# Attention's value products on four 32-column tiles of TensorE in place of two 64-column tiles

## The chip, the cores and the metric

The kernel runs on one core of a Trainium2 chip. The metric is the device time of one execution, in microseconds (us). A core has five engines that run side by side and wait for one another by semaphores: PE (TensorE, the matrix engine; its weight loads have a row of their own, PEld), DVE (VectorE), ACT (ScalarE), POOL (GpSimd) and SP (SyncE, which here issues the DMAs).

## The reference

The input `x` has 64 batches of 256 nodes with 512 features; `adj` is a graph on the 256 nodes. Two layers follow each other, and each adds its result to its input and normalises over the features.

```
# layer 0: one step on the graph
out = deg * (x @ Wi.T + b) + adj @ (x @ Wj.T)
h   = layernorm(x + out)
# layer 1: attention with 8 heads of 64 features, masked by the graph
q, k, v = split_heads(h @ Wq.T + bq), ..., ...
attn = softmax(where(adj == 0, -inf, q @ k.T / 8))
out  = layernorm(h + (attn @ v) @ Wo.T + bo)
```

The change touches the product `attn @ v` alone. It is computed here as exponentials times `v`, and divided by the sums of the exponentials afterwards.

## The kernel before

**Groups and slots.** Batches are worked on in pairs; 32 pairs make 32 groups `g`. Within a group the attention runs over 8 units `w`: `i, pr = divmod(w, 4)` gives the batch of the pair and a pair of heads. The loop takes two units at a time, which I call a slot, so a group has four slots. In all groups but the last, a slot runs on PE in this order, written out by hand and kept as written (`in_order`, `keep_in_program_order`):

1. `values(g, w)` and `values(g, w + 1)`: the products into the tile `pav`. This is what the change edits.
2. `divide`: four products of `ones` with `pk` into `den`, which sum the exponentials of each head over the keys.
3. `scores`: the products of `qT` and `kT` into `ps` for the next units, in the first three slots. In the fourth, the projections of the group's end (`st`) follow.
4. Pieces of the next group's layer 0 (`po`, `pa`), which fill PE while the other engines make the exponentials.

All matrix products go through one helper, so the profile gives them line L290, and they are told apart by the tile that they write. A product of 32-bit floats stands in the trace as two `MATMUL` and two `LDWEIGHTS` records.

**The tile shapes.** PE's array of 128 by 128 can be used as several smaller arrays. The profile writes the shape in use as rows*columns:

- `po`, `st` and `pa` use the whole array, `128*128`.
- `pav` uses `128*64`: head `j` of the pair writes partitions `64j` to `64j + 63`, so the heads `j = 0` and `j = 1` stand on two tiles of the array. One unit is 2 chunks of keys (`kc`) times 2 heads: 4 products, each with 128 keys as rows, 64 features as columns, and 256 queries that stream.
- `den` uses `128*32`: its four products of 32 columns stand on four tiles, placed by `tile_position=(0, q * R)` with `R = 32`.
- `ps` uses `64*128`: two tiles one above the other, since a head has 64 features.

**What hangs on these products.** ACT makes the exponentials `pe` (L813) after DVE has added the mask (L809), and POOL adds the two halves of `pe` to `pk` (L816), which `den` reads. When `pav` of a slot is complete, ACT copies it to `aoT` (L853). When `den` is complete, DVE takes its reciprocal `rden` (L886). SP then issues 8 DMAs that spread `rden` over the partitions, and POOL multiplies `aoT` by it one slot later (L848). `pav` has one PSUM bank (`ps_v`, 1 buffer). `den` shares three banks with `po` and `st` (`ps_m`).

**The group's end.** After the fourth slot's `den` come the output projection (`st<-factor,aoT` and `st<-factor,oS`), and then the query, key and value projections of the next group (`st<-hT`, `st<-hS`). DVE turns `h` there (`hT<-hB`, a transpose of data that came back by DMA), and sums blocks of it.

**The last group** has no next layer 0 to mix in. It takes single units, with `scores` between them, and for its last two units `divide_at_once` computes `den` on `128*64` tiles.

Of the kernel before, what the change touches and what calls it, by code (L numbers as in the profile page):

```python
# [16 lines left out]
P = 128  # L17
# [207 lines left out]
def unshifted_path(ctx, tc, flag, x, adj, wiT, wjT, b0, wqT, bq, wkT, bk, wvT, bv, woT, bo, out):  # L225
# [18 lines left out]
    NT = N // P  # L244
    NC = D // P
    DH = 64
    R = 32
# [30 lines left out]
    def value_bank(name):  # L278
        return ps_v.tile([P, 512], F32, tag="av", name=name)


    def in_order(ins):

        tc.keep_in_program_order(ins)
# [4 lines left out]
    def matmul(*args, **kw):  # L289
        in_order(nc.tensor.matmul(*args, **kw))  # L290
# [33 lines left out]
    xT, xS, hT, hS, qT, kT, vv, aoT, oS = ({} for _ in range(9))  # L324
# [310 lines left out]
    def pair_blocks(m, tag):  # L635

        s = p1.tile([P, 4, 2, N], F32, tag=tag, name=tag)
        return left_blocks(m[:, 0:2, 0:N], m[:, 2:4, 0:N], m[:, 0:2, N:2 * N], m[:, 2:4, N:2 * N], s)
# [33 lines left out]
    def second_late(steps):  # L672
        return [steps[0], steps[2], steps[1], *steps[3:]]
# [30 lines left out]
    def qk_steps(g, store, tag, bias, diff, early=False):  # L704

        def new_store():
            store[g] = p1.tile([P, NC, NB * N], F32, tag=tag, name=tag)

        def place(i, j):
            return store[g][:, 2 * j:2 * j + 2, i * N:(i + 1) * N]  # L710

        def biased(b):
            def evict(dst, ps):
                for m in range(2):
                    nc.scalar.activation(dst[:, m, :], ps[:, m, :], AF.Identity, bias=b[:, m:m + 1], scale=1.0)
            return evict

        def last(dst, ps, addend):
            for m in range(2):
                nc.vector.scalar_tensor_tensor(dst[:, m, :], ps[:, m, :], diff[:, m:m + 1],  # L720
                                               addend[:, m, :], ALU.add, ALU.add)

        return qkv_steps(g, True, new_store, place, biased(bias), biased(diff), last, early)
# [98 lines left out]
    pavs = {}  # L822
# [7 lines left out]
    def values(g, w):  # L830
        i, pr = divmod(w, NC)
        if w == 0:
            aoT[g] = p1.tile([P, NC, NB * N], F32, tag="aoT", name="aoT")
            oS[g] = pair_blocks(aoT[g], "oS")
        pp = w % 2
        if pp == 0:
            pavs[g] = value_bank("pav").rearrange("p (r q) -> p r q", r=2)
        pe, _ = made[g, w]
        for kc in range(NT):
            for j in range(2):  # L840
                h0 = (2 * pr + j) * DH
                matmul(pavs[g][j * DH:(j + 1) * DH, pp, :], vv[g][:, i, kc, h0:h0 + DH], pe[:, j, kc, :],
                       start=(kc == 0), stop=(kc == NT - 1))

    def multiply():
        while products:
# [73 lines left out]
    def order_of(name):  # L920
        return [(name, n) for n in RIGHT]

    for g in range(-1, NG - 1):
        o, q, k, v = (order_of(name) for name in ("wo", "wq", "wk", "wv"))
# [18 lines left out]
    p, q = l0_steps(0), l0_steps(1)  # L943
# [42 lines left out]
    for g in range(NG - 1):  # L986
# [4 lines left out]
        for w in range(2, NB * NC, 2):  # L991
            values(g, w - 2)
            values(g, w - 1)
            multiply()
            divide_two(g, w - 1)
            scores(g, w)()
            if w == 4:
                run(work[2])
            later = scores(g, w + 1)
            later()  # L1000
            run(work[w // 2 if w < 4 else w // 2 + 1])
        w = NB * NC - 2
        values(g, w)
        values(g, w + 1)
        multiply()
        o = o_steps(g)
        q = second_late(qk_steps(g + 1, qT, "qT", bq_sb, bqd))
# [20 lines left out]
    g = NG - 1  # L1028
# [89 lines left out]
```

## Time and profile before

| | |
|---|---|
| median of 3 runs | 3089.34 us (3087.36 to 3089.66) |
| the profiled execution's own time | 3086.33 us |
| its span in the trace | 3084.3 us |
| PE busy | 3055.9 us, 99% of the span, 14598 `MATMUL` records |
| PEld busy | 2122.5 us, 69% |
| DVE, ACT, POOL busy | 71%, 32%, 49% |
| DMA engines busy | 48.9% |
| granted TensorE clock | 0.999 |

The profile comes from one execution, in which the time outside the span was 2.0 us. Its time is 3.0 us below the median of the three timed runs. Busy time of a group of instructions is the union of their durations: the records of `pav` last 386 ns each on average, but since they overlap, 2048 of them cover only 250.1 us. So the starts of records tell what a product costs on PE, and the mean duration of one does not.

### The profile page before, as it was taken

What the parts mean: (1) busy time and instruction counts of PE and PEld (TensorE: products, weight loads), DVE (VectorE), ACT (ScalarE), POOL (GpSimd) and SP (SyncE); (2) the same over time, 40 slices, a digit from 0 to 9 for tenths busy, and PEclk for the clock granted to TensorE, in tenths of its full rate; (3) what the DMA queues carried; (4) which work ended last, traced back from release to release, by engine and by line L of the source; (5) the groups of instructions that cost most, each with busy time, mean ns of one, the idle gap of its engine ahead of it and who ended that gap; (6) DMA issues with size and microseconds to landing.
All of it is one profiled execution on the core that took longest, in us unless ns stands there. A gap on an engine that the chain in (4) does not pass through costs nothing. (4 is left out here: it accounts for less than half of the span.)

```text
span 3084.3 us, 42714 instructions
## 1 busy us (share of the span) xinstructions
PE 3055.9 (99%) x14598; PEld 2122.5 (69%) x14598; DVE 2176.4 (71%) x3298; ACT 974.7 (32%) x1861; POOL 1519.8 (49%) x1255
## 2 busy tenths in 40 slices
PE   7999999999999999999999999999999999999998
PEld 4667766677766777666776667776677766677665
DVE  6777677766777667777667676677766777767765
ACT  2323333323333333332233332333332333323332
POOL 2544445544546445464454554454544546445453
PEclk9999999999999999999999999999999999999999
DMA  7355544455444555445554445544455444555333
GB/s 258 121 147 157 168 124 129 135 158 166 143 127 124 159 169 152 119 131 151 159 167 120 126 141 159 166 140 126 126 157 170 148 121 128 156 161 164 118 110 99
DMA packets 410395, 447.28 MB, mean 145 GB/s; under 512 B 40896, under 2 KB 300224, under 8 KB 409792
## 3 DMA queue, kind: packets, MB, share of 16 engines
q1 hardware_dynamic: 410176, 444.50, 48.9%
q8 instruction: 120, 1.97, 0.3%
q14 instruction: 99, 0.81, 0.1%
HBM read 340.79 MB, written 70.25 MB: 133 GB/s over the span
## 5 line engine op out<-in xcount | busy, mean ns | idle before, releaser
L461 POOL TENSOR_TENSOR rstd<-ve,mhalf 128x1 f32<-128x1 f32 x256 | 140.6, 553 | 706.2 <-DVE below L459 706.2
L816 POOL TENSOR_TENSOR pk<-pe 128x512 f32<-128x512 f32 x256 | 322.6, 1276 | 327.4 <-ACT pe L813 327.3
L290 PE MATMUL po<-w,xS 128*128 128x512 f32 x1024 | 463.0, 599 | 0.4 <-DVE xS L478 0.4
L290 PE MATMUL st<-hS,factor 128*128 128x256 f32 x2048 | 453.1, 379 | 1.6 <-DVE u L689 1.2
L290 PEld LDWEIGHTS st<-hS,factor 128*128 128x128 f32 x2048 | 387.9, 190 | 56.6 <-DVE u L689 1.7
L813 ACT ACTIVATE pe<-pe 128x1024 f32<-128x1024 f32 x256 | 270.8, 1058 | 379.0 <-DVE pe L809 379.0
L290 PE MATMUL po<-w,xT 128*128 128x512 f32 x768 | 351.9, 601 | 13.4 <-DVE xT L485 10.9
L290 PE MATMUL st<-hT,factor 128*128 128x256 f32 x1536 | 352.4, 379 | 0.7 <-ACT hT L626 0.7
L290 PEld LDWEIGHTS po<-w,xS 128*128 128x128 f32 x1024 | 189.7, 190 | 236.3 <-issue 207.2
L809 DVE TENSOR_TENSOR pe<-ps,maskT 128x1024 f32<-128x1024 f32 x256 | 297.9, 1194 | 35.3 <-PE ps L290 35.3
L290 PEld LDWEIGHTS st<-hT,factor 128*128 128x128 f32 x1536 | 291.5, 190 | 42.3 <-ACT hT L626 0.9
L886 DVE RECIPROCAL rden<-den 128x256 f32<-128x256 f32 x127 | 222.6, 1753 | 92.1 <-PE den L290 89.0
L887 POOL TENSOR_TENSOR rtot<-rtot,rden 128x256 f32<-128x256 f32 x127 | 106.9, 841 | 329.4 <-DVE rden L886 329.4
L290 PEld LDWEIGHTS po<-w,xT 128*128 128x128 f32 x768 | 143.6, 191 | 180.7 <-issue 162.5
L290 PE MATMUL ps<-qT,kT 64*128 64x256 f32 x2048 | 264.9, 392 | 0.0
L290 PE MATMUL pav<-pe,v_sb 128*64 128x256 f32 x2048 | 250.1, 386 | 1.9 <-ACT pe L813 1.8
L290 PEld LDWEIGHTS pav<-pe,v_sb 128*64 128x64 f32 x2048 | 135.3, 136 | 154.1 <-issue 95.5
L290 PEld LDWEIGHTS ps<-qT,kT 64*128 64x128 f32 x2048 | 184.3, 186 | 78.2 <-issue 51.3
L744 DVE TENSOR_TENSOR xh<-st,xh 128x512 f32<-128x512 f32 x186 | 144.5, 777 | 131.7 <-PE st L290 131.7
L290 PE MATMUL st<-factor,hS 128*128 128x256 f32 x1024 | 234.8, 382 | 0.0
L290 PE MATMUL st<-factor,oS 128*128 128x256 f32 x992 | 224.2, 379 | 0.0
L290 PEld LDWEIGHTS st<-factor,hS 128*128 128x128 f32 x1024 | 191.9, 190 | 35.4 <-issue 10.6
(115 smaller groups left out, 4633.5 us busy)
## 6 DMA issues: line engine op xcount, KB each, us to landing
xB<-in_x_dram SPq DMA_DIRECT2D x256, 128.0 KB, 3.9
xh<-in_x_dram SPq DMA_DIRECT2D x64, 512.0 KB, 4.3
factor<-wq SPq DMA_DIRECT2D x128, 256.0 KB, 4.2
factor<-wk SPq DMA_DIRECT2D x128, 256.0 KB, 2.8
factor<-wv SPq DMA_DIRECT2D x128, 256.0 KB, 2.7
spread<-rden SPq DMA_DIRECT2D x1016, 32.0 KB, 1.9
factor<-wo SPq DMA_DIRECT2D x124, 256.0 KB, 3.2
h_cols<-xh SPq DMA_DIRECT2D x124, 256.0 KB, 2.8
```

Source lines behind the costliest of these rows:

```text
L290: in_order(nc.tensor.matmul(*args, **kw))
L461: nc.gpsimd.tensor_tensor(rstd, ve, mhalf, ALU.pow)
L744: nc.vector.tensor_add(dst, src, dst)
L809: nc.vector.tensor_add(pe.rearrange("p j t q -> p j (t q)"), ps.rearrange("p j t q -> p j (t q)"), maskT.rearrange("p t q -> p (t q)").uns ...
L813: in_order(nc.scalar.activation(flat, flat, AF.Exp, scale=QSCALE, accum_out=etot[:, NB * g + i, pr:pr + 1]))
L816: nc.gpsimd.tensor_tensor(pk, pe[:, :, 0, :], pe[:, :, 1, :], ALU.add)
L886: nc.vector.reciprocal(rden, den)
L887: nc.gpsimd.tensor_tensor(rtot, rtot, rden, ALU.add)
```

## The change

In `values`, the loop over the two heads becomes a loop over four blocks of 32 columns. Block `q` holds 32 of the 64 features of head `q // 2`, and writes partitions `32q` to `32q + 31` of `pav`.

```
         for kc in range(NT):
-            for j in range(2):
-                h0 = (2 * pr + j) * DH
-                matmul(pavs[g][j * DH:(j + 1) * DH, pp, :], vv[g][:, i, kc, h0:h0 + DH], pe[:, j, kc, :],
-                       start=(kc == 0), stop=(kc == NT - 1))
+            for q in range(P // R):
+                d0 = 2 * pr * DH + q * R
+                matmul(pavs[g][q * R:(q + 1) * R, pp, :], vv[g][:, i, kc, d0:d0 + R], pe[:, q // 2, kc, :],
+                       start=(kc == 0), stop=(kc == NT - 1), tile_position=(0, q * R))
```

A unit now has 8 products of 32 columns where it had 4 of 64, each with the same 256 queries streaming; the two blocks of a head stream the same exponentials. Over the kernel, 1024 products become 2048. In the built programs nothing else differs: PE has every other product at its place, and DVE, ACT, POOL and SP have the same instructions in the same order. The edit reaches the last group as well, where `divide_at_once` keeps its 64 columns.

## The prediction

> **What bounds the kernel now.** I read the page's first part, then who PE waits for, then the timeline of one slot.
>
> ```profile
> span 3084.3 us, 42714 instructions
> PE 3055.9 (99%) x14598; PEld 2122.5 (69%) x14598; DVE 2176.4 (71%) x3298; ACT 974.7 (32%) x1861; POOL 1519.8 (49%) x1255
> ...
> L290 PE MATMUL pav<-pe,v_sb 128*64 128x256 f32 x2048 | 250.1, 386 | 1.9 <-ACT pe L813 1.8
> ```
>
> PE is busy for 99% of the span. The row of `pav`, the edited products, shows 1.9 us of idle time before 2048 records. The list of PE's waits adds up to 20 us, and its largest line is the kernel's start:
>
> ```profile
> PE po L290 <- DVE xT L485: 10.9, 2, 8.1
> PE pt_h L293 <- ACT xh L467: 2.3, 2, 1.2
> PE pav L290 <- ACT pe L813: 1.8, 2, 1.0
> ```
>
> So PE sets the time, and what its stream sheds or gains, the kernel sheds or gains, until another engine comes late. But a busy PE need not be streaming. The timeline of one slot (columns: start, length, then the group; the number after x counts records) shows what lies between starts:
>
> ```profile
> 1052.71 0.59 PE L290 MATMUL po<-w,xS 128*128 128x512 f32 x1
> 1053.24 1.95 PE L290 MATMUL pav<-pe,v_sb 128*64 128x256 f32 x16
> 1055.11 0.64 PE L290 MATMUL den<-pk,ones 128*32 128x256 f32 x8
> 1055.68 2.00 PE L290 MATMUL ps<-qT,kT 64*128 64x256 f32 x16
> ...
> ```
>
> And a stretch of whole-array products, then the end of the last group:
>
> ```profile
> 1006.16 1.89 PE L290 MATMUL st<-factor,aoT 128*128 128x256 f32 x8
> 1007.89 5.34 PE L290 MATMUL st<-factor,oS 128*128 128x256 f32 x24
> ...
> ```
>
> ```profile
> 3063.74 1.08 PE L290 MATMUL pav<-pe,v_sb 128*64 128x256 f32 x8
> 3064.66 1.03 PE L290 MATMUL den<-pk,ones 128*64 128x256 f32 x8
> ```
>
> Take starts, not lengths. Eight `st` records take 1007.89 - 1006.16 = 1.73 us, 216 ns each: 256 columns streamed twice. The 16 records of `pav` take 1055.11 - 1053.24 = 1.87 us. They run in pairs, one for each half of the array, so they make 8 steps, and 8 x 0.216 = 1.73 us. The 8 records of `den` run four at once, make 2 steps (0.43 us), and take 0.57. So `pav` and `den` each carry 0.14 us that is no streaming. In the last group, `pav` and `den` both stand on 64 columns: 3064.66 - 3063.74 = 0.92 us for 4 steps (0.86), only 0.06 over, though output, weights and data all change there.
>
> The single records of the slot tell the extra time apart (ns, from start to start; outside the last group each repeats within 2 ns):
> - Within `pav`: 267 for the first step, then 216 for each. Products of one step start 7 apart.
> - From the last start of `pav` to the first of `den`: 309 in all 127 places, so 93 more than a step. The same 93 stands from `den` to `ps` and from `st` to `ps`, and 90 from `ps` to `po`: wherever the shape changes. From `pav` to the 64-column `den` it is 210.
> - Within `den`: 240 for its first step.
>
> **What the Trainium skill says.** "TensorEngine Tiling (Array Packing)", section Key Properties: "Changing tiling mode (not just tile) drains the TensorE". The trace agrees: 93 ns at each change of shape, nothing without one. "TensorE: Matmul & The Clock Gate", section LDWEIGHTS (loading the stationary operand): a load takes as long as its columns divided by 1.2 per ns, so 53 ns for 64 columns and 27 for 32 as estimates from that page. The trace's first steps are longer by 51 and 24 ns: after a change the second load finds no stream to hide behind. The same page, section The mechanism, has tiles of the array running at once, about 4 ns apart; here it is 7. Its section Measured speedup vs the span model reports 2.38 times for three tiles of 32 columns, one product each; no run here shows that, nor a long run of fours.
>
> **The change, part by part.**
>
> *Streaming.* Each product covers a quarter of the array's columns where it covered half, and there are twice as many: 8 products of two records per unit, 32 records per slot, in fours 8 steps as before. If four run at once, streaming costs the same 8 x 216 ns; nothing is gained there.
>
> *First step.* After the change of shape from `po`, the exposed load is of 32 columns: 240 instead of 267. That removes 27 ns.
>
> *From pav to den.* Both are now `128*32`: no drain. Step to step is 216 where last `pav` to first `den` was 309. As the last record of a four starts 20 ns after its first, and of a pair 7, count from first records: 316 before, 216 after. That removes 100 ns.
>
> *Den's first step* has its loads hidden behind the last `pav` step: 216 instead of 240. That removes 24 ns.
>
> *From den to ps* (or to `st` in the fourth slot): the change of shape stays, 309.
>
> The sum is 27 + 100 + 24 = 151; by whole slots, from `pav`'s first start to `ps`'s: 2446 before; after, 240 + 8 x 216 + 20 + 309 = 2297, so 149 ns less. I take 149. With 31 groups of 4 slots: 124 x 0.149 = **18.5 us**. The last group I cost at nothing: two of its three earlier `den` blocks wait for `pk` halfway, PE waits 1.8 us for exponentials there, and its final `den` of 64 columns now needs a change of shape that it did not have (about 0.1 us lost). Bounds: 0.4 us gained, 0.2 lost.
>
> *Instructions.* 2048 `MATMUL` and 2048 `LDWEIGHTS` records come in. PE must issue 8 instructions per 216 ns, 27 ns each. PE's sequencer shows how fast it can: two of its semaphore records with 16 matrix instructions between them start 125 ns apart at 995.1 us (and in many other groups), under 8 ns each. It stands up to 34 instructions ahead of PE, and four tiles need about 16. Instruction fetch: 1.97 + 0.81 MB for 42714 instructions, 65 bytes each, so 0.27 MB more beside 447 MB. I cost both at nothing.
>
> *Who comes late next.* No other engine has an instruction more, less or moved, SP's and POOL's queues and their DMAs included, and no wait is added. PE only arrives sooner, by 0.13 us at `den` and 0.15 after it. What it needs there, from the end of the producer to PE's start now: `pk` (L816) for `den` in the third slot 0.31 us, in other slots over 4; exponentials for `pav` over 0.70. So `pk` keeps 0.18 us; if it were late, `den`, and `ps` and `po` behind it, would wait. The shortest answer of another engine that PE's starts show is 0.055 us after a DVE add (L744), so 0.18 suffices.
>
> `rden` (L886) starts 0.446 us after `den`'s last start in three slots, DVE having been idle over 0.6: it moves along with PE. In the fourth, DVE is busy with `hT<-hB` until then; `rden` stays where it is, falls 0.13 us behind PE, and with it its DMAs and the multiply (L848). What hangs on that has 0.39 us at its shortest (`st<-factor,aoT`) and 0.66 (`st<-factor,oS`). At the group's end the closest is `st<-hS` behind the add of L744, with mostly 0.22 us; DVE idles on PE several times between, so it starts anew from PE. Over a group of 95.0 us, DVE is busy 67: it can follow 0.6 us less. Cover gone in one place per group would cost 31 x 0.1 = 3 us.
>
> **The sum.** From the profiled execution's 3086.3: 3067.8. That execution is 3.0 us under the median of the runs shown, so I set the saving against the median: 3089.3 - 18.5 = **3070.8 us**.
>
> **The rivals.**
>
> *Four don't run at once for long (slower).* `den` shows only 2 steps of four, with its operands loaded beforehand. If the array fed only two of `pav`'s tiles at a time, each of its 8 steps would become two: 8 x 0.216 = 1.73 us more in a slot, 128 x 1.73 - 18.5 = +203 us, 3292 us. It decides from 149 / 8 = 19 ns per step on: with 235 ns in place of 216 the gain is gone. It may be milder: if the loads of every step are exposed, 24 ns as in `den`'s first, that is paid on 8 more steps, 8 x 24 - 149 = 43 ns more in a slot, +5 us, 3094.7. For it: nothing in the trace shows a third step of four. Against: `den`'s second step of four streams at full pace, and with 64 columns the loads, twice as long, are hidden from the second step on.
>
> *The drain stays (no change).* If the 93 ns came from the change of output or operand, and not of shape, `pav` to `den` would keep it, with the exposed load of `den`. Left are the 27 ns of the first step, less 13 for the wider fan: 124 x 0.014 = 2 us, 3087.6. Against: the 64-column pair in the last group (210) and `st`'s blocks, which change all of these for nothing.
>
> *The gain is partly eaten.* The third slot or the group's end waits as bounded above: 3074, still faster.
>
> **How the numbers follow.** About 0.2%, 6.2 us, is what a measurement of this kernel can tell from no change: 3083.2 to 3095.5. Main case, with partial losses (steps of four up to 12 ns longer among them): 0.83, faster. Drain stays: 0.05, the same. Steps longer by 12 to 25 ns, exposed loads among them: 0.04, which also lands within 0.2%. Two at a time, or anything over 25 ns a step: 0.08, slower. The range holds the main case: below, 3067.5, for two us of spread between runs and the last group's gain; above, 3079, for the 3 us of partial waits and some 5 ns per step (5 us). The slow rivals are left out of it.
>
> **What would show it.** In the timeline of the same slot, `pav` reads `128*32` and x32, and from its start to `den`'s are 1.75 us (1.87 now), to `ps`'s 2.30 (2.44). The group period falls from 95.0 to 94.4 us. A first `den` 309 ns after the last `pav` would show the drain kept; steps above 216 within `pav`, the slower rival; a PE row waiting for `pk` (L816), the third. I am wrong if the steps of four are longer than 235 ns, or if PE's waits grow by more than 12 us.

## The result and the profile after

The median fell from 3088.93 us (3087.36 to 3089.66, 4 runs) to 3068.39 us (3067.99 to 3071.78, 4 runs). The ratio is 0.9937 with a 95% interval of 0.9919 to 0.9954, so 14 to 25 us less. The profiled execution took 3068.79 us, with a span of 3066.9 us.

The head of the page, and the row of `pav`:

```profile
span 3066.9 us, 46810 instructions
PE 3036.6 (99%) x16646; PEld 2124.6 (69%) x16646; DVE 2178.3 (71%) x3298; ACT 974.1 (32%) x1861; POOL 1519.5 (50%) x1255
...
L290 PE MATMUL pav<-pe,v_sb 128*32 128x256 f32 x4096 | 248.4, 382 | 1.9 <-ACT pe L813 1.9
```

PE has 2048 records more and 19.3 us less of busy time; DVE, ACT and POOL have the instructions that they had, and PE is still the engine at 99%. The row of `pav` alone would mislead. Its busy time fell by 1.7 us only, because most of the gain (100 of the 151 ns of the prediction's parts) lies between `pav` and `den` rather than in either.

The timeline of the same slot shows it (start, length, group; read the starts):

```profile
1047.84 0.59 PE L290 MATMUL po<-w,xS 128*128 128x512 f32 x1
1048.36 1.94 PE L290 MATMUL pav<-pe,v_sb 128*32 128x256 f32 x32
1050.11 0.61 PE L290 MATMUL den<-pk,ones 128*32 128x256 f32 x8
1050.65 2.00 PE L290 MATMUL ps<-qT,kT 64*128 64x256 f32 x16
```

From `pav`'s start to `den`'s is 1.75 us where it was 1.87, and to `ps`'s 2.29 where it was 2.44 (the prediction shows these lines of before). By single records it is 2296 ns against 2447, and each of the 124 slots of the first 31 groups is within 1 ns of that. The time from one group's first `pav` to the next's fell from a median of 95.00 us to 94.39.

PE's waits hardly grew:

```profile
PE po L290 <- DVE xS L477: 9.3, 1, 9.3
PE po L290 <- DVE xT L485: 2.8, 1, 2.8
...
PE pav L290 <- ACT pe L813: 1.9, 3, 1.0
...
PE st L290 <- DVE xh L744: 0.3, 1, 0.3
```

The whole list adds up to 22.5 us where it was 20.0. Of these 2.5 us more, 1.8 lie in the kernel's start, to which the first two lines belong, and 0.6 in the last group. Between 200 and 3000 us PE has a single wait in the list, the 0.3 us of the last line, where it was 0.2 before. `pk` (L816) is not in the list.

The span's 17.4 us are made up of three parts. The 31 group periods together are 18.6 us shorter. The start up to the first `pav` took 103.63 us where it took 102.71, which costs 0.9 us; in the other kernels below it varied from 102.3 to 105.5, so this is no effect of the change. From the last group's first `pav` to the end took 0.3 us longer (42.76 for 42.50), and part of that is the change's doing:

```profile
3046.36 1.07 PE L290 MATMUL pav<-pe,v_sb 128*32 128x256 f32 x16
3047.36 1.08 PE L290 MATMUL den<-pk,ones 128*64 128x256 f32 x8
3048.37 1.13 PE L290 MATMUL po<-wo_sb,aoT 128*128 128x512 f32 x2
```

`pav` and `den` now differ in shape at the kernel's last unit: 1.00 us from start to start, where it was 0.92. PE also waits 0.5 us for `aoT` (L848) in this group, as it did not before; whether that is the change's doing is not shown.

### The profile page after: what moved, and what is told of

The parts are those of the page before. It is cut to its first block, busy times and chain, and to the rows that moved or that the text cites. A ratio compares the mean times of both kernels' runs of the same rounds, so it can differ in the third digit from the quotient of the medians.

```text
span 3066.9 us, 46810 instructions
## 1 busy us (share of the span) xinstructions
PE 3036.6 (99%) x16646; PEld 2124.6 (69%) x16646; DVE 2178.3 (71%) x3298; ACT 974.1 (32%) x1861; POOL 1519.5 (50%) x1255
## 5 line engine op out<-in xcount | busy, mean ns | idle before, releaser
L816 POOL TENSOR_TENSOR pk<-pe 128x512 f32<-128x512 f32 x256 | 323.1, 1278 | 322.2 <-ACT pe L813 322.2
L290 PE MATMUL pav<-pe,v_sb 128*32 128x256 f32 x4096 | 248.4, 382 | 1.9 <-ACT pe L813 1.9
L290 PEld LDWEIGHTS pav<-pe,v_sb 128*32 128x32 f32 x4096 | 119.8, 110 | 164.3 <-issue 95.4
```

What stands on the lines that cost most here:

```text
L816: nc.gpsimd.tensor_tensor(pk, pe[:, :, 0, :], pe[:, :, 1, :], ALU.add)
```

## The experiments

My theory was that the gain is the change of shape between `pav` and `den`, with the exposed first loads, and nothing else. The first rival said that products on 32 columns are cheaper in themselves. The second said that the gain depends on what PE can look ahead to.

### One more change of shape: only the first unit on 32 columns

```
+        C = R if pp == 0 else DH
         for kc in range(NT):
-            for q in range(P // R):
+            for q in range(P // C):
...
-                       start=(kc == 0), stop=(kc == NT - 1), tile_position=(0, q * R))
+                       start=(kc == 0), stop=(kc == NT - 1), tile_position=(0, q * C))
```

> As after, but only the first unit of each slot (even w) takes its value products on 32 columns, the second (odd w) on 64; the result is the reference's. So a slot has the shapes 128*128, 128*32, 128*64, 128*32 (den): one change of shape more than before and two more than after. If changes of shape and exposed first loads make the difference: from pav's first start to ps's first 240 + 2 x 216 + 20 + 309 + 267 + 2 x 216 + 7 + 309 + 240 + 20 + 309 = 2585 ns, against 2447 before and 2296 after. That is 124 x 0.138 = 17 us more than before: about 3106 us. If products on 32 columns were themselves cheaper than on 64, half of the units would bring half of the gain: about 3079 us.

Measured: 3106.51 us (3103.66 to 3110.62), ratio 1.0059 (1.0042 to 1.0076) to before, 17.5 us more. A slot took 2584 ns from `pav` to `ps`. Half of the units were on 32 columns, and the kernel was slower than with none.

```profile
1058.36 2.08 PE L290 MATMUL pav<-pe,v_sb 128*32 128x256 f32 x24
1060.37 0.64 PE L290 MATMUL den<-pk,ones 128*32 128x256 f32 x8
1060.94 0.92 PE L290 MATMUL ps<-qT,kT 64*128 64x256 f32 x6
```

(The form named in the first row is that of its first records; the row holds 16 records of 32 columns and 8 of 64.) Between the two units the trace has 309 ns from the last start to the first, within the 305 to 310 of the other changes of shape. The first rival falls.

### The change of shape moved: only the second unit on 32 columns

The same edit with `pp == 1`.

> As after, but only the second unit of each slot (odd w) takes its value products on 32 columns, the first on 64; the result is the reference's. The change of shape stands between the two units instead of between pav and den: as many changes as before. If changes of shape and exposed first loads make the difference: 267 + 2 x 216 + 7 + 309 for the first unit, 240 + 7 x 216 less the one step within den (4 steps of pav and 1 of den in one shape: 240 + 4 x 216) + 20 + 309 for the rest, 2448 ns from pav's first start to ps's, the same as before: about 3089 us. If products on 32 columns were themselves cheaper: half of the gain, about 3079 us.

Measured: 3090.30 us (3088.54 to 3092.71), ratio 1.0004 (0.9995 to 1.0013) to before. A slot took 2447 ns, as before. In the timeline the drain has gone from `pav`'s end into its middle, so that the gap from the last start of `pav` to `den` alone (196 ns for 309) would look like a gain; the start of `ps` tells that there is none:

```profile
1055.51 2.08 PE L290 MATMUL pav<-pe,v_sb 128*64 128x256 f32 x24
1057.41 0.61 PE L290 MATMUL den<-pk,ones 128*32 128x256 f32 x8
1057.95 0.92 PE L290 MATMUL ps<-qT,kT 64*128 64x256 f32 x6
```

(The form named in the first row is that of its first records; the row holds 8 records of 64 columns and 16 of 32.)

### The shape alone: den on 64 rows

```
-                matmul(den[q * R:(q + 1) * R, :], ones[:, :R], pks[pp][:, j, :], start=True, stop=True,
+                matmul(den[q * R:(q + 1) * R, :], ones[:DH, :R], pks[pp][:DH, j, :], start=True, stop=True,
```

> After, with the four products of den reading only the first 64 of the 128 partitions of pk and ones: it leaves half of the keys out of the sums. Products, columns, steps and order are those of after; only the tile's shape is another, 64*32 in place of 128*32. If the gain between pav and den is the shape that they share: the last start of pav to the first of den 309 again (196 in after), den's first step 240 from first to fifth record (216), so 1555 + 309 + 260 + 309 = 2433 ns from pav's first start to ps's (2296 in after): 124 x 0.137 = 17 us more than after, about 3085 us, though no product has changed its number of columns. If the gain were den's place right after products of 32 columns, whatever the rows: 3068 us as after.

Measured: 3088.90 us (3086.80 to 3091.87), ratio 1.0000 (0.9991 to 1.0009) to before. The whole gain is gone, although `pav` is as in the changed kernel and `den` has the same columns, steps and place:

```profile
1054.75 1.93 PE L290 MATMUL pav<-pe,v_sb 128*32 128x256 f32 x32
1056.61 0.64 PE L290 MATMUL den<-pk,ones 64*32 64x256 f32 x8
1057.18 0.70 PE L290 MATMUL ps<-qT,kT 64*128 64x256 f32 x4
```

The last start of `pav` to the first of `den` is 309 ns again (196 in after), and `den`'s first step 240 (216). The slot took 2430 ns, the group period 94.93 us. By the periods this costs 16.7 us of the 18.8 that the change saved in them. What is left is 17 ns in a slot: `pav`'s first step is 27 ns shorter than before, the fan of its last step (the spread of the starts that run together) is 13 ns wider, and `ps` follows 306 ns after `den` where it was 309. That makes 2 us, which these medians can't tell. So the rows of the shape count as its columns do.

### The order of the products within a unit

```
-        for kc in range(NT):
-            for q in range(P // R):
+        for q in range(P // R):
+            for kc in range(NT):
```

> As after, with the two loops in values exchanged (for q outside, for kc inside), so that the two products of one tile follow each other in the program, and the first product of the fourth tile stands 6 products (24 instructions) behind the first of the first tile, instead of 3 products. The result is the reference's. If PE starts a product as soon as its tile is free, as far as it stands ahead in the program (up to 34 instructions by the trace of before): the four still run at once, 8 steps in a slot, 3068 us as after. If products started only in the order of the program, a tile's four records would go one after the other and only the border of two tiles would overlap: 13 steps for a unit in place of 4, 18 x 0.216 = 3.9 us more in a slot, about 3570 us.

Measured: 3074.29 us (3073.66 to 3077.69), ratio 0.9956 (0.9939 to 0.9972) to before, 5.9 us more than after by the medians. The four do run at once: the first records of the four tiles start within 40 ns, though the fourth tile's stands 24 instructions behind the first's in the program. So there the order of the program doesn't bind the start. But it isn't free:

```profile
1048.42 1.97 PE L290 MATMUL pav<-pe,v_sb 128*32 128x256 f32 x32
1050.17 0.65 PE L290 MATMUL den<-pk,ones 128*32 128x256 f32 x8
1050.76 0.70 PE L290 MATMUL ps<-qT,kT 64*128 64x256 f32 x4
```

`den` starts as early as in after (1.75 us), and `ps` 37 ns later. The four products of a step start 13 ns apart instead of 7, and from the sixth step on one of them 30 ns late; the last of `den` carries that fan to the next change of shape, which has to wait for it. 4 x 37 = 148 ns in a group, as its period says (94.54 us for 94.39), 4.6 us in 31 groups. Both theories of the expectation missed this size: I had put the first at no cost. The spacing fits how far the products stand apart in the program: 7 ns with 4 instructions from one to the next, 13 with 8; other distances were not tried. Why one is late by 30 from the sixth step on is open.

### Changes of shape elsewhere: the graph step after both scores

In the third slot `pa` (`128*128`) stood between two stretches of `ps` (`64*128`).

```
             scores(g, w)()
-            if w == 4:
-                run(work[2])
             later = scores(g, w + 1)
             later()
-            run(work[w // 2 if w < 4 else w // 2 + 1])
+            if w == 4:
+                run(work[3][4:5] + work[2] + work[3][:4] + work[3][5:])
+            else:
+                run(work[w // 2 if w < 4 else w // 2 + 1])
```

> After, with the third slot in another order: the products pa of the graph step, which stand between the two units' scores, come after both scores and one step of po. The result is the reference's. It takes a change of shape out twice (128*128 for pa between two ps of 64*128) and one exposed first load of ps. If changes of shape are pure loss on PE's path wherever they stand: 90 + 89 + 104 = 283 ns less per group, 31 x 0.283 = 8.8 us less than after, about 3060 us. Against that, pa starts some 2.6 us later, and with it the normalisation, the DMA to DRAM and back and the turn of hT for the first batch of the pair, which has 2.5 to 3.2 us to spare in the trace of after. If that is used up in most groups, DVE comes late at the fourth slot and PE waits at the group's end: then 3068 us or more.

Measured: 3060.79 us (3058.06 to 3061.68), ratio 0.9906 (0.9889 to 0.9923) to before. The group period is 94.01 us, 386 ns less than after where I expected 283. After, then this kernel, from `ps` to `pav` in the third slot:

```profile
1061.94 1.14 PE L290 MATMUL ps<-qT,kT 64*128 64x256 f32 x8
1063.01 0.50 PE L290 MATMUL pa<-hi,graph 128*128 128x512 f32 x1
...
1065.07 1.14 PE L290 MATMUL ps<-qT,kT 64*128 64x256 f32 x8
1066.14 3.70 PE L290 MATMUL po<-w,xT 128*128 128x512 f32 x8
1069.77 1.50 PE L290 MATMUL pav<-pe,v_sb 128*32 128x256 f32 x24
```

```profile
1059.43 2.00 PE L290 MATMUL ps<-qT,kT 64*128 64x256 f32 x16
1061.36 1.98 PE L290 MATMUL po<-w,xT 128*128 128x512 f32 x4
1062.78 0.79 PE L290 MATMUL pa<-hi,graph 128*128 128x512 f32 x1
...
1065.06 1.88 PE L290 MATMUL po<-w,xT 128*128 128x512 f32 x4
1066.86 1.93 PE L290 MATMUL pav<-pe,v_sb 128*32 128x256 f32 x32
```

7.83 us became 7.43. The 104 ns that I missed are those of one more first load: `pa` after `ps` exposed one as well, and after `po` doesn't. With 90 + 89 + 104 + 104 = 387 the sum closes. The feared delay of the first batch stayed within what was to spare: its `hB`, which had landed 2.5 to 3.2 us ahead of its turn, now lands 0.3 to 1.1 us ahead. The second batch's `hB` comes late in a few groups, here as in before. By the lists of waits, DVE waits for it 0.8 us in all in before, 0.9 in after and 3.2 here, of which 2.0 in one group, so the 31 periods together are 9.6 us shorter than in after, where 31 x 0.386 makes 12.0. Since `first32`, a slower kernel, has 2.5 us of these waits too, it is not shown that the new order brings them.

### The exposed loads: scores on narrower tiles

```
-        for kc in range(NT):
-            for j in range(2):
...
+        C = DH
+        for kc in range(NT):
+            for c in range(P // C):
+                for j in range(2):
+                    rows = slice(j * DH, (j + 1) * DH)
+                    k0 = n0 + kc * P + c * C
+                    matmul(ps[c * C:(c + 1) * C, j, kc, :], kT[g][rows, pr, k0:k0 + C],
+                           qT[g][rows, pr, n0:n0 + N], start=True, stop=True, tile_position=(j * DH, c * C))
```

> After, with the scores' products split in two: 64*64 tiles, four at once (two heads, two blocks of 64 keys), where ps had 64*128 and two at once. The result is the reference's. It doubles the products of ps as the change doubled those of pav, but takes no change of shape away. If the exposed first load goes by its columns and the fan by the products per step: first step 266 for 320, last step of the fan 20 for 7, so 40 ns less for each stretch of ps; 5 stretches in a group, 31 x 5 x 0.040 = 6.2 us less than after, about 3062 us. If a first load isn't exposed by its columns, but the whole step after a change of shape is a fixed cost: the fan alone, 31 x 5 x 0.013 = 2 us more, about 3070 us.

Measured: 3064.14 us (3063.24 to 3066.61), ratio 0.9921 (0.9904 to 0.9937) to before. The first step of `ps` is 267 ns for 321, each stretch 40 ns shorter (1887 for 1927), the group period 200 ns (94.19 us), all as the first theory says. By the medians it is 4.3 us less than after, and by the sum of the 31 periods 4.0, where 31 x 0.200 makes 6.2: DVE waits 3.0 us for `hB` in this trace, 0.9 in that of after.

The same with `C = R`:

> After, with the scores' products split in four: 64*32 tiles, eight at once. The result is the reference's. By the same sum: first step 243 for 320, fan of eight 47 for 7, 36 ns less for each stretch of ps: 31 x 5 x 0.036 = 5.6 us less than after, about 3063 us, if PE sees far enough ahead: eight products are 32 instructions, and 34 is the farthest that the trace of before shows. If it does not, some of the eight start late in each step; if only four run at once, each of the 8 steps of a slot becomes two, 31 x 4 x 8 x 0.216 = 214 us more, about 3280 us.

Measured: 3067.54 us (3064.59 to 3068.72), ratio 0.9929 (0.9912 to 0.9945) to before. Each stretch and the group period are those of `scores64` (1888 ns, 94.19 us): the first load is shorter still, and the fan of eight, 46 ns, takes it back. All eight ran at once. The median shows less of it: in the profiled execution the start is 1.8 us and the last group 1.6 us longer than in after. The start varies anyway. In the last group of this trace PE waits 2.1 us for `pk` (L819 here) ahead of two blocks of `den`, which the list of after doesn't have. Why `pk` comes late there is open.

### The last group, and all of it together

```
-            for j in range(2):
-                matmul(den[j * DH:(j + 1) * DH, pp, :], ones[:, :DH], pk[:, j, :], start=True, stop=True)
+            for q in range(P // R):
+                matmul(den[q * R:(q + 1) * R, pp, :], ones[:, :R], pk[:, q // 2, :], start=True, stop=True,
+                       tile_position=(0, q * R))
```

> pa_later, and in the last group divide_at_once takes its sums on four tiles of 32 columns in place of two of 64 (the same 4 steps), so that den has the shape of the value products ahead of it. The result is the reference's. If a change of shape and its exposed load are what the last group lost with the change: 93 + 51 ns less between the last pav and po, and 13 more for the wider fan of the last step, 0.13 us in all at the trace's end; the time itself as pa_later, 3060.7 us, since 0.13 us can't be told by it. If the longer last group of after has another reason, the stretch from the last pav's first start to po's stays as it is.

Measured: 3060.63 us (3056.20 to 3061.56), ratio 0.9903 (0.9887 to 0.9920) to before. From the last `pav` to `po`:

```profile
3038.48 1.07 PE L290 MATMUL pav<-pe,v_sb 128*32 128x256 f32 x16
3039.36 1.05 PE L290 MATMUL den<-pk,ones 128*32 128x256 f32 x16
3040.34 1.13 PE L290 MATMUL po<-wo_sb,aoT 128*128 128x512 f32 x2
```

1864 ns, against 2015 in `pa_later`, 2014 in after and 1878 before. So these 0.14 us of the last group's loss were the change of shape that the edit had brought there, and they can be had back. The time doesn't tell it, as expected.

> pa_later_last32 together with scores64; the result is the reference's. With pa_later there are 4 stretches of ps in a group: 31 x 4 x 0.040 = 5.0 us less than pa_later_last32, about 3056 us, if what is taken out of PE's path goes on adding up. If another engine has become the bound by then (pk for the third slot's den, the turn of hT), less than half of that, 3058.5 us or more.

Measured: 3053.04 us (3052.32 to 3053.15), ratio 0.9882 (0.9866 to 0.9899) to before. This is the fastest version, 15.3 us below after by the medians. The group period is 93.85 us, 160 ns below `pa_later` for four stretches of 40, which makes 5.0 us. The median fell further, by 7.6 us below `pa_later_last32`; the runs of that kernel spread over 5.4 us, and DVE waits 4.9 us for `hB` in its trace, 3.2 in this one. PE is still 99% busy:

```profile
span 3051.1 us, 50921 instructions
PE 3020.5 (99%) x18702; PEld 2081.2 (68%) x18702; DVE 2183.8 (72%) x3298; ACT 980.5 (32%) x1861; POOL 1521.4 (50%) x1255
```

## Why the prediction was right

**The bound.** PE set the time, and it passed its saving on. Of the 18.8 us that 31 periods less by 0.607 us make, 18.6 arrived in the sum of the periods; the rest is a few groups that wait for the DMA of `hB`, as a few did before.

**The terms of the sum.** Streaming stayed at 216 ns a step through all 8 steps. The first step is 240 ns (267 before), the 27 of the prediction. From `pav` to `den` it is 196 from the last start, 216 from the first of a four: the 100 ns. `den`'s first step is 216 (240 before): the 24 ns. Its weight loads now start 214 ns ahead of their products, where they started 2 ns ahead. From `den` to `ps` it stayed 309. The slot took 2296 ns where I had worked out 2297, and the group period, predicted as 94.4 us, is 94.39. What `second32`, `first32` and `den_rows64` add is the cause: the time follows the changes of shape, and neither the number of columns (but for the exposed first load) nor the number of products. That the drain goes by shape is what the Trainium skill says ("TensorEngine Tiling (Array Packing)", section Key Properties), without a price; here it is 90 to 93 ns, plus the first load that it exposes: 24, 51 and 104 ns for 32, 64 and 128 columns. That the 90 to 93 ns are a drain is the page's word: the traces show their size, and that it is the same ahead of loads of 32, 64 and 128 columns.

**Who comes late next.** In the third slot, the first product of `den` that reads the later `pk` starts 0.186 us after `pk` is made. The prediction left 0.18, counted to `den`'s first product, which is 0.174 now. No product of PE waits for it. But the prediction looked past the weight loads: those of the second unit's sums do wait for `pk`. They start 0.05 us after its end in each of the 31 groups, 0.135 us ahead of their products, where in the other slots it is 0.214. The path through `rden` in the fourth slot did not reach PE either.

**The rivals.** Four products do run at once over many steps, and their loads are hidden, so the slower rival has no case. The drain did not stay. The waits of the last rival hardly grew: DVE waits 0.9 us for `hB` in the whole trace, where it waited 0.8.

**The last group.** I cost it at nothing, within 0.4 us gained and 0.2 lost. In the trace it became 0.27 us longer, past that bound. The change of shape that it gained cost 0.14 us (1878 to 2014 ns), where I had put 0.1, and was undone in `pa_later_last32`. The rest can't be put down to the change, since the last group takes from 42.5 to 44.4 us in the kernels here.

**The size.** The forecast was 3070.8 us and the median 3068.39. The medians differ by 20.5 us, the traces' spans by 17.4 and the forecast was 18.5: the interval of 14 to 25 us holds all three, and no experiment here points at a further gain of the change. Most of the way from 17.4 to 20.5 is the profiled execution of before, which was 2.6 us faster than its median. That the median came within 2.4 us of the forecast is in part luck, since the four runs of after alone spread over 3.8 us; the slot's 2296 ns for 2297 are not.

## What to carry to other kernels

Where a tuned PE stream mixes array shapes, read the starts in the timeline and subtract the streaming: what is left at each border is a drain and an exposed first load (here 90 to 93 ns and 24 to 104), and both can be taken out without less arithmetic, by giving neighbours the same shape or by putting pieces of one shape side by side. Splitting a product into narrower tiles cost PE no streaming time here, with as many columns running at once and the pieces that run together next to each other in the program; what it cost is a wider fan at the next change of shape, 13 ns for four products in place of two. Check the whole stretch up to the next border that didn't move; a drain that only wanders into a row looks like a gain at the row's end.

## What the runs showed of the hardware that I had not expected

- Products on four tiles started within 40 ns (60 from the sixth step on) even with the fourth 24 instructions behind the first (`q_outer`), and eight within 47 ns on `64*32` tiles, each step still 216 ns (`scores32`).
- The spread of their starts fits their distance in the program: 7 ns for 4 instructions, 13 for 8. The last start of the fan counts at the next change of shape, which makes the narrowest tile no better than the middle one (`scores32` and `scores64`, 1888 and 1887 ns).
